# A four-layer graph network on one core: layer 3 planned among layer 2, preparation in two parts, loads by need

## The chip, the cores and the metric

The kernel runs on one core of one Trainium2 chip. The metric is the device time of one execution in microseconds (us); the median of three executions of the kernel before is 1182.61 us.

The core's engines work side by side, each through its own queue in order: TensorE (PE, matmuls, with its weight loads shown as PEld), VectorE (DVE), ScalarE (ACT), GpSimd (POOL) and SyncE (SP), which here only issues transfers (DMAs). TensorE reads from SBUF and writes to PSUM, of which the kernel uses eight banks of 128 x 512 f32.

## The reference, cut to what matters

32 graphs of 512 nodes with 128 features pass through four layers; all graphs share one adjacency matrix, and no graph depends on another. Every layer is `x = x + layer(relu(layernorm(x)))`.

```python
def _L0(x, adj, ...):            # attention over scores of node pairs, softmax over the other axis
    h = x @ others_weight
    ...
    out = einsum('bik,bkl->bil', att, h) + x @ self_weight
def _L1(x, A, ...):              # attention, then an aggregation over A and two dense steps
    h = x @ Wp + bp
    attn = softmax(where(A <= 0, min, leaky(s_src[:, :, None] + s_dst[:, None, :])))
    h_gat = relu(layernorm((attn * A) @ h) * gat_g + gat_b)
    z = ((1 + eps) * h_gat + A @ h_gat) @ W1 + b1
    return relu(relu(layernorm(z) * mlp_g + mlp_b) @ W2 + b2 + h_gat)
def _L2(h, adj, W, a, bias):     # attention
    Wh = h @ W
    attention = softmax(where(adj > 0, leaky(f1[:, :, None] + f2[:, None, :]), NEG))
    return elu(attention @ Wh + bias)
def _L3(x, adj, W, e, bias):     # one matrix for all graphs
    A = softmax(where(adj > 0, e[0][cumsum(adj > 0) - 1], NEG))
    return (A * eye) @ (x @ W[0]) + (A * (1 - eye)) @ (x @ W[1]) + bias
```

Layer 3's matrix A depends on the adjacency and on e alone, not on x. It is computed once, and it needs a long chain: the rank of every edge, the look-up of e by rank, a softmax.

## The kernel before, in words

**A graph.** x stays in SBUF for all 32 graphs (`xs`, 128 partitions x 4 chunks of 128 nodes). `preln` normalises a graph: statistics on VectorE (`st`, `mv`, `nmean`), the reciprocal deviation `rstd` and the scaled `xn` on GpSimd, four transposes on TensorE (`pt`), the relu into `hT` on ScalarE. `layer0` projects (`proj` to `h`), sends a small piece of `h` through four tiny DMAs on SP's queue to bring pair scores to other partitions (`u`), repeats a row (`prow`), takes maxima on VectorE, exponentials on ScalarE, scales (`hs`) and multiplies (`po`). `layer1` and `layer2` share `attend`: row `prow`, four `y` with the mask (line 574, VectorE), a leaky step and an exponential for each (lines 596 and 604, ScalarE), 16 transposes of `y` (line 375, TensorE), copies `pT` and 16 matmuls `po` (line 624). `layer1` goes on with an aggregation over `adjTe` (`pg`, line 795) and two dense steps (`pz`, `px`). `layer3` is short on every engine but TensorE: `own` (line 845), `p` (line 522), four groups of five matmuls (`po`, lines 856 and 860), a sum `yo` and the store of the result.

**The plan.** The order of instructions on each engine isn't written by hand. Every step is given to a `Plan` (line 94) as an operation with an engine, an estimated length and what it reads and writes; operations of one graph in one layer form a chain. `Plan.run` (line 136) simulates the engines with these lengths and emits the operations one by one: of the operations that could begin first on an engine (within `SLACK`), it takes the one with the smallest turn. A chain's turn is its begin, which grows by a `gap` from chain to chain (line 107), plus `STRETCH` times the length of the way to the operation. At most `WINDOW` = 7 chains beyond the oldest unfinished one may run (line 160). Tiles come from rooms with a fixed number of places, the eight PSUM banks among them. The emitted order is binding for each engine (line 194).

**Order of the chains.** The preamble (line 390: loads of x and the adjacency, layer 0's weights, masks), then all 32 graphs of layer 0, all of layer 1, all of layer 2, all of layer 3 (line 1161).

**The preparation.** `prepare` (line 871) makes what the later layers need and no graph owns: the centred weights and score columns of layer 1 and 2, the biases in three bf16 terms (`terms`, line 952), the adjacency with its diagonal (`adjTe`), the parameter rows, and layer 3's matrix: `maskT`, `pn` (line 1017), `num`, `pb` (line 1032), `in_row`, `pg` (line 1083), `pd` (line 1105), the softmax, the transposes `pt_att` into `offT` (line 1152) and the diagonal `pr` into `adiag_rep` (line 1156). It is one chain outside the window, a filler: its turn is `FILLED` = 1e6 for every operation, so that any operation of a graph that can begin at the same time goes first; and it must leave two PSUM banks free.

**Transfers.** SP's queue carries the x loads (eight ahead: `AHEAD`, lines 393 to 397, then one by each layer-0 graph, line 637), the preparation's loads, the four `u` transfers of each layer-0 graph (line 648) and the stores. ScalarE's queue carries three loads at the start (lines 398 to 400). A transfer in the plan takes its issue, a delay of 2.2 and, if it has a `load`, time on one shared bus.

Of the kernel before, what the change touches and what calls it, by code (L numbers as in the profile page):

```python
# [33 lines left out]
P = 128  # L34
# [3 lines left out]

WINDOW = 7

AHEAD = 8


PE, DVE, ACT, POOL, SP, ACTQ = "PE", "DVE", "ACT", "POOL", "SP", "ACTQ"

DELAY = {PE: 0.25, DVE: 0.15, ACT: 0.2, POOL: 0.15, SP: 2.2, ACTQ: 2.2}

SLACK = 0.05

STRETCH = 4.0  # L50

FILLED = 1e6


class Room:
# [29 lines left out]
class Operation:  # L85
    def __init__(self, engine, length, emit, chain, slots):
        self.engine, self.length, self.emit, self.chain, self.slots = engine, length, emit, chain, slots
        self.after, self.missing = [], 0
        self.ready = 0.0
        self.load = 0.0  # L90
        self.way = 0.0


class Plan:
# [7 lines left out]
        self.chains = []  # L102
        self.begin = 0.0

    def chain(self, gap=0.0, filler=False):

        self.chains.append([0, filler, FILLED if filler else self.begin])
        self.begin += gap

    def op(self, engine, length, emit, reads=(), writes=(), load=0.0):  # L110
        slots = list(dict.fromkeys(v.slot for v in (*reads, *writes) if v.slot is not None))
        k = len(self.chains) - 1
        op = Operation(engine, length, emit, k, slots)
        op.load = load
# [12 lines left out]
        for n in needs:  # L127
            n.after.append(op)
            if n.chain == k:
                op.way = max(op.way, n.way + n.length + DELAY[n.engine])  # L130
        op.turn = (self.chains[k][2] + STRETCH * op.way, len(self.ops))
        op.missing = len(needs)
        self.chains[-1][0] += 1
        self.ops.append(op)

    def run(self):
        tc, nc = self.tc, self.tc.nc
        idle = dict.fromkeys(DELAY, 0.0)
        bus = 0.0
        ready = {e: [] for e in DELAY}  # L140
        for op in self.ops:
            if not op.missing:
                ready[op.engine].append(op)
        left = [n for n, _, _ in self.chains]
        normal = [k for k, (_, filler, _) in enumerate(self.chains) if not filler]
        order = {k: i for i, k in enumerate(normal)}
        oldest = 0
        last = {}
        traced = nc.cur_bb.bb.instructions
        seen = len(traced)  # L150
        for _ in range(len(self.ops)):
            while oldest < len(normal) and not left[normal[oldest]]:
                oldest += 1
            best = None
            for engine, ops in ready.items():
                could = []
                for op in ops:
                    k = op.chain
                    filler = self.chains[k][1]
                    if not filler and order[k] >= oldest + WINDOW:  # L160
                        continue
                    begin = max(idle[engine], op.ready)
                    new = [s for s in op.slots if s.tile is None]
                    rooms = {}
                    for s in new:
                        rooms[s.room] = rooms.get(s.room, 0) + 1
                    for room, n in rooms.items():
                        if len(room.free) < n + (room.reserve if filler else 0):
# [12 lines left out]
            ready[op.engine].remove(op)  # L181
            for s in op.slots:
                if s.tile is None:
                    s.room.free.remove(min(s.room.free))
                    s.tile = s.room.make(s.name)
            end = begin + op.length
            idle[op.engine] = end
            done = end + DELAY[op.engine]
            if op.load:
                bus = max(done, bus) + op.load  # L190
                done = bus
            op.emit()
# [25 lines left out]
def kernel(  # L218
# [137 lines left out]

    def load(engine, dst, src, writes, size=0.0):
        q = nc.sync if engine is SP else nc.scalar
        op(engine, 0.45, lambda: q.dma_start(dst(), src), writes=writes, load=size)

    def load_x(b):
        load(SP, lambda: xs[:, b], x[b].rearrange("(c p) f -> p c f", p=P), [v_x[b]], 1.0)
# [27 lines left out]
    plan.chain()  # L390
    wt_o = value(spare, "wt_o")
    v_att = Value()
    load_x(0)
    for ib in range(C):
        load(SP, lambda ib=ib: bias[:, ib, :], adj[blk(ib), :], [v_adj[ib]], 1.0)
    for b in range(1, AHEAD):
        load_x(b)
    load(ACTQ, lambda: wt_o.t[:, 0, :], l0_wo, [wt_o], 0.25)
    load(ACTQ, lambda: att, l0_att.rearrange("(t p) o -> p (t o)", p=P), [v_att])
    load(ACTQ, lambda: wts[:, W_S, :], l0_ws, [v_wts[W_S]], 0.25)  # L400
    v_w0b = Value()
    score_weights(lambda: wt_o.t[:, 0, :], wt_o, att, v_att, w0_ext[:, P:P2], v_w0)
    copy_op(DVE, 0.15, lambda: w0_ext[:, 0:P], lambda: wt_o.t[:, 0, :], [wt_o], [v_w0b])
# [232 lines left out]
    def layer0(b):  # L636
# [12 lines left out]
                        u.own[up * 64 : up * 64 + 64, :, k : k + 1], h[0].t[k:P:2, up:C:2, P + k : P + k + 1]  # L649
                    )  # L650

        op(SP, 1.8, emit_pair, h, [u])
        ls = Value()

        def emit_ls():
# [185 lines left out]
    def layer3(b):  # L841
# [26 lines left out]
        op(SP, 0.5, lambda: nc.sync.dma_start(out[b].rearrange("(c p) f -> p c f", p=P), yo.t), [yo], [Value()])  # L868


    def prepare():
        def dve(length, emit, reads, writes):
            op(DVE, length, emit, reads, writes)

        wt_p, wt_1, wt_l2, row_p, row_1 = (value(spare, n) for n in ("wt_p", "wt_1", "wt_l2", "row_p", "row_1"))
        v_a1, v_a2, v_e, v_eps = Value(), Value(), Value(), Value()

        def line(v):
            return v.rearrange("(p o) -> p o", o=1)
# [14 lines left out]
            load(SP, lambda n=n: mlp_gb[:, n : n + 1], line(v), [v_mlp])  # L894
        for n, v in enumerate((l1_gg, l1_gb, l1_b2, l2_bias, l3_bias)):
            load(SP, lambda n=n: rows[:, n, :], all_rows(v), [v_rows], 0.25)
        for n, w in ((W_2, l1_w2), (W_30, l3_w[0]), (W_31, l3_w[1])):
            load(SP, lambda n=n: wts[:, n, :], w, [v_wts[n]], 0.25)
        load(SP, lambda: e_col, l3_e.rearrange("o (t p) -> p (o t)", p=P), [v_e])
        load(SP, lambda: e_last, l3_e[:, NE - 1 : NE].to_broadcast([P, 1]), [v_e])  # L900

        for ib in range(C):
            dve(0.31, lambda ib=ib: nc.vector.tensor_scalar(
# [67 lines left out]

        dve(0.15, lambda: nc.vector.tensor_scalar(rows[:, B_L2, :], rows[:, B_L2, :], 1.0, None, ALU.add), [], [v_rows])
        dve(0.15, lambda: nc.vector.tensor_scalar(rows[:, B_L3, :], rows[:, B_L3, :], -1.0, None, ALU.add), [], [v_rows])

# [181 lines left out]
        turn_op(lambda k: pr3.t[:, k, :], lambda k: adiag[:, k : k + 1].to_broadcast([P, P]), v_diag, [pr3])  # L1156
        copy_op(ACT, 0.49, lambda: adiag_rep, lambda: wide(pr3.t), [pr3], [v_adiag_rep])

    plan.chain(filler=True)
    prepare()  # L1160
    for layer, gap in ((layer0, 6.6), (layer1, 13.3), (layer2, 7.6), (layer3, 5.9)):
        for b in range(B):
            plan.chain(gap)
            layer(b)
    plan.run()


# [31 lines left out]
```

## Time and profile before

| what | value |
|---|---|
| executions of the kernel before | 1182.61, 1182.65, 1181.53 us |
| the profiled execution | 1182.39 us, of which the span from first to last instruction is 1180.3 us |
| TensorE busy | 1109.0 us (94% of the span) |
| VectorE busy | 961.3 us (81%) |
| ScalarE busy | 665.4 us (56%) |
| GpSimd busy | 670.2 us (57%) |
| mean granted TensorE clock | 0.975 |
| chain of waits that ended last | TensorE 60%, VectorE 28%, ScalarE 4%, GpSimd 3% |
| x load, 256 KB | 32 issues, 4.0 us to landing |
| `u` transfer, 0.5 KB | 128 issues, 1.8 us to landing |

The profile is of one execution. A busy time is the sum of the times in which an engine had an instruction under way; on TensorE neighbouring matmuls overlap, so that the distance from one start to the next tells more than a length. The rows of the slices cut the span into 40 equal parts of 29.5 us and give the busy share of each in tenths. The table of stretches gives, for each engine, the busy time and in brackets the number of instructions; the last three columns are the granted TensorE clock, the share of the DMA engines and GB/s. In a timeline, the bracket at the end of a row is the time in which the engine sat idle before it and what it waited for.

The stages by the timeline: layer 0 to about 243 us, layer 1 to about 747, layer 2 to about 977, layer 3 to the end.

### The profile page before, as it was taken

To read this page: it belongs to the slowest core of one execution; us is meant where nothing else is said; L and a number is where in the kernel's file an instruction comes from. 1 tells how busy PE (TensorE), PEld (TensorE's weight loads), DVE (VectorE), ACT (ScalarE), POOL (GpSimd) and SP (SyncE) were. 2 spreads that over 40 slices of the span, in tenths; PEclk is the share of its full clock that TensorE was granted. 3 is DMA by queue.
4 is the path that set the end of the run, shared out by engine and by line. 5 is a ranking of instruction groups with operands and counts; after the bars stand their busy time and mean duration, and the time that the engine had idled before them with its cause. 6 is when DMAs were issued, how large, how long until landed. Compare 5 with 4: busy or idle time off the path is not lost.

```text
span 1180.3 us, 25261 instructions
## 1 busy us (share of the span) xinstructions
PE 1109.0 (94%) x8682; PEld 1002.6 (85%) x8683; DVE 961.3 (81%) x3854; ACT 665.4 (56%) x1588; POOL 670.2 (57%) x1040
## 2 busy tenths in 40 slices
PE   4899999977999999999999999997999997999998
PEld 3899999976778878788878878697999996999998
DVE  5999999966988898898998888999999997444431
ACT  2555555415747655666556767598999992122221
POOL 5444444530464664645674565746677686777761
PEclk8899999988999999999999999999999997999999
DMA  7111210000000000000000000000000000111111
GB/s 194 29 37 38 46 20 2 2 1 1 2 1 1 2 1 1 2 1 1 2 1 1 2 1 2 1 2 1 2 1 2 2 1 10 46 46 46 46 46 54
DMA packets 56911, 20.50 MB, mean 17 GB/s; under 512 B 21584, under 2 KB 56272, under 8 KB 56784
## 3 DMA queue, kind: packets, MB, share of 16 engines
q1 hardware_dynamic: 56224, 18.76, 6.5%
q8 instruction: 69, 1.13, 0.4%
q14 instruction: 58, 0.48, 0.1%
q10 hardware_dynamic: 560, 0.13, 0.1%
HBM read 10.43 MB, written 8.39 MB: 16 GB/s over the span
## 4 chain that ended last, share of the span: by engine, by line
PE 60%; DVE 28%; ACT 4%; POOL 3%; issue 2%; DMA 2%; SPq 0%; DVEq 0%; ACTq 0%; POOLq 0%
PE po L624 11%; PE po L860 10%; PE pt L375 7%; PE po L749 7%; PE pg L795 6%; DVE y L574 5%; PE proj L544 4%; DVE st L461 4%; DVE pT L368 3%; PE po L856 2%; PE p L522 2%; DVE pT L613 2%; ACT y L604 2%; PE prow L375 2%; PE px L522 2%
## 5 line engine op out<-in xcount | busy, mean ns | idle before, releaser
L624 PE MATMUL po<-h,pT 128*128 128x128 f32 x2048 | 249.5, 278 | 17.3 <-DVE pT L368 14.3
L624 PEld LDWEIGHTS po<-h,pT 128*128 128x128 f32 x2048 | 239.6, 194 | 26.1 <-DVE pT L368 17.6
L497 POOL TENSOR_SCALAR xn<-xs,nmean,rstd 128x128 f32<-128x128 f32 x512 | 229.2, 462 | 46.3 <-DVE yo L867 39.4
L596 ACT ACTIVATE y<-y,h 128x512 f32<-128x512 f32 x256 | 165.5, 718 | 48.6 <-DVE rmax L574 48.4
L604 ACT ACTIVATE y<-y,nmax 128x512 f32<-128x512 f32 x256 | 181.9, 719 | 11.6 <-DVE nmax L587 10.2
L506 ACT ACTIVATE hT<-pt 128x512 f32<-128x512 f32 x128 | 76.0, 595 | 174.2 <-DVE own L845 90.1
L477 POOL TENSOR_TENSOR rstd<-ve,mhalf 128x4 f32<-128x4 f32 x160 | 162.9, 1018 | 13.3
L574 DVE CUSTOM_DVE_ANT_0 y<-prow,bias 128x512 f32<-128x512 f32 x256 | 161.1, 681 | 4.3 <-PE prow L375 4.3
L375 PEld LDWEIGHTS pt<-ident,y 128*128 128x128 f32 x1024 | 115.9, 142 | 34.1 <-ACT y L604 21.0
L375 PE MATMUL pt<-ident,y 128*128 128x128 f32 x1024 | 132.8, 276 | 9.0 <-ACT y L604 7.6
L860 PE MATMUL po<-h,offT 128*128 128x128 f32 x1024 | 136.8, 277 | 0.0
L475 POOL TENSOR_SCALAR ve<-mv 128x4 f32<-128x4 f32 x160 | 34.6, 216 | 167.6 <-DVE mv L463 142.4
L860 PEld LDWEIGHTS po<-h,offT 128*128 128x128 f32 x1024 | 126.3, 194 | 0.0
L795 PE MATMUL pg<-adjTe,hg 128*128 128x512 f32 x256 | 126.2, 593 | 0.0
L544 PE MATMUL proj<-w_ext,hT 128*128 128x130 f32 x768 | 110.2, 283 | 2.0 <-ACT hT L506 1.9
L366 ACT COPY h<-proj 128x260 f32<-128x260 f32 x192 | 66.7, 370 | 79.6 <-PE proj L544 63.2
L461 DVE BATCH_NORM_STATS2 st<-xs 128x6 f32<-128x128 f32 x512 | 110.6, 277 | 0.3 <-DMA xs<-in_x_dram 0.3
L544 PEld LDWEIGHTS proj<-w_ext,hT 128*128 128x128 f32 x768 | 100.1, 198 | 6.9 <-ACT hT L506 3.0
L776 POOL TENSOR_TENSOR rstd<-ve,mhalf 128x4 f32<-128x4 f32 x32 | 32.7, 1023 | 109.2 <-DVE ve L769 102.7
L613 DVE TENSOR_TENSOR pT<-pt,adjT 128x512 f32<-128x512 f32 x128 | 81.3, 680 | 15.5 <-PE pt L375 15.3
L375 PE MATMUL pt<-ident,xn 128*128 128x128 f32 x512 | 86.0, 283 | 5.5 <-POOL xn L497 3.9
L375 PEld LDWEIGHTS pt<-ident,xn 128*128 128x128 f32 x512 | 63.4, 143 | 21.8 <-POOL xn L497 16.2
(190 smaller groups left out, 2135.0 us busy)
## 6 DMA issues: line engine op xcount, KB each, us to landing
xs<-in_x_dram SPq DMA_DIRECT2D x32, 256.0 KB, 4.0
out_dram<-yo SPq DMA_DIRECT2D x32, 256.0 KB, 2.2
u<-h SPq DMA_DIRECT2D x128, 0.5 KB, 1.8
bias<-in_adj_dram SPq DMA_DIRECT2D x4, 256.0 KB, 4.8
wts<-in_L_gnn_W_dram SPq DMA_DIRECT2D x3, 64.0 KB, 2.6
rows<-in_L_gnn_bias_dram SPq DMA_DIRECT2D x2, 64.0 KB, 3.3
wt_o<-L_gnn_others_weight_dram ACTq DMA_DIRECT2D x1, 64.0 KB, 4.7
wts<-n_L_gnn_self_weight_dram ACTq DMA_DIRECT2D x1, 64.0 KB, 5.1
```

Source lines behind the costliest of these rows:

```text
L375: nc.tensor.transpose(dst(k), src(k), ident)
L461: nc.vector.bn_stats(st[:, c, :], src(c))
L477: nc.gpsimd.tensor_tensor(rstd.own, ve, mhalf, ALU.pow)
L497: nc.gpsimd.tensor_scalar(xn.t[:, c, :], src[:, c, :], nmean.own[:, c : c + 1], rstd.own[:, c : c + 1], ALU.add, ALU.mult,)
L544: nc.tensor.matmul(p[:, c, :], lhsT=column(hT, 2 * k + c), rhs=w_ext, start=(b3 is None), stop=(b3 is None or c == 1),)
L574: nc.vector.tensor_tensor_reduce(wide(y[ib].t), wide(prow.t), bias[:, ib, :], 1.0, LOWEST, ALU.add, ALU.max, rmax.own[:, ib : ib + 1],)
L596: nc.scalar.activation(yw, yw, AF.Prelu, alpha=0.2, bias=h[0].t[:, ib, P : P + 1])
L604: nc.scalar.activation(yw, yw, AF.Exp, bias=nmax.own[:, ib : ib + 1], accum_out=ssum[0].own[:, ib : ib + 1])
L613: op(DVE, 0.6, lambda ib=ib, pt=pt, pT=pT: nc.vector.tensor_mul(pT.t, pt.t, weights[:, :, blk(ib)]), [pt, *v_weights], [pT])
L624: nc.tensor.matmul(po[ib].t[:, ib, :], lhsT=pT.t[:, jb, :], rhs=h[0].t[:, jb, 0:P], start=(jb == 0), stop=(jb == C - 1),)
L795: nc.tensor.matmul(wide(pg.t), lhsT=hg.t[:, nb, :], rhs=adjTe[:, nb, :], start=(nb == 0), stop=(nb == C - 1))
L860: nc.tensor.matmul(po[ib].t[:, ib, :], lhsT=offT[:, jb, blk(ib)], rhs=h1.t[:, jb, :], start=False, stop=(jb == C - 1),)
```

## The change

Four things are changed, all of them in what the plan is told; no operation's computation is touched.

1. The chains of layers 2 and 3 are interleaved: layer 3 of graph b follows layer 2 of graph b + 4 (`LAG`), with gaps of 7.0 and 6.0 instead of 7.6 and 5.9.
2. The preparation becomes two chains. `prepare` (all but layer 3's matrix) has the turn `PREPARED` = 40, `prepare_last` (layer 3's weights, e and the matrix) keeps `FILLED`. Neither counts in the window.
3. The loads: the three loads of ScalarE's queue are declared earlier, six graphs of x are loaded ahead instead of eight, and the plan now has eight transfer lanes: a transfer must wait until the one eight before it has landed. The `u` transfers take four lanes, a store takes a lane and time on the bus.
4. The first six chains of graphs are `RAMP` = 4 times as far apart in their begins.

```diff
-AHEAD = 8
+AHEAD = 6
+LANES = 8
-FILLED = 1e6
+PREPARED, FILLED = 40.0, 1e6
+RAMP, LAG = 4.0, 4
...
-    def chain(self, gap=0.0, filler=False):
-        self.chains.append([0, filler, FILLED if filler else self.begin])
+    def chain(self, gap=0.0, turn=None, name=""):
+        self.chains.append([0, turn is not None, self.begin if turn is None else turn, name])
         self.begin += gap
...
-        op.turn = (self.chains[k][2] + STRETCH * op.way, len(self.ops))
+        _, beside, begin, _ = self.chains[k]
+        op.turn = (begin + (0.0 if beside else STRETCH * op.way), len(self.ops))
...
+        lanes = [0.0] * LANES
...
                     begin = max(idle[engine], op.ready)
+                    if op.transfers:
+                        begin = max(begin, lanes[op.transfers - 1])
...
             if op.load:
                 bus = max(done, bus) + op.load
                 done = bus
+            if op.transfers:
+                lanes = lanes[op.transfers :] + [done] * op.transfers
...
+    load(ACTQ, lambda: wt_o.t[:, 0, :], l0_wo, [wt_o], 0.25)
     load_x(0)
+    load(ACTQ, lambda: att, l0_att.rearrange("(t p) o -> p (t o)", p=P), [v_att])
     for ib in range(C):
         load(SP, lambda ib=ib: bias[:, ib, :], adj[blk(ib), :], [v_adj[ib]], 1.0)
+    load(ACTQ, lambda: wts[:, W_S, :], l0_ws, [v_wts[W_S]], 0.25)
     for b in range(1, AHEAD):
         load_x(b)
-    load(ACTQ, lambda: wt_o.t[:, 0, :], l0_wo, [wt_o], 0.25)
-    load(ACTQ, lambda: att, l0_att.rearrange("(t p) o -> p (t o)", p=P), [v_att])
-    load(ACTQ, lambda: wts[:, W_S, :], l0_ws, [v_wts[W_S]], 0.25)
...
-        op(SP, 1.8, emit_pair, h, [u])
+        op(SP, 1.8, emit_pair, h, [u], transfers=4)
...
-        for n, w in ((W_2, l1_w2), (W_30, l3_w[0]), (W_31, l3_w[1])):
-            load(SP, lambda n=n: wts[:, n, :], w, [v_wts[n]], 0.25)
-        load(SP, lambda: e_col, l3_e.rearrange("o (t p) -> p (o t)", p=P), [v_e])
-        load(SP, lambda: e_last, l3_e[:, NE - 1 : NE].to_broadcast([P, 1]), [v_e])
+        load(SP, lambda: wts[:, W_2, :], l1_w2, [v_wts[W_2]], 0.25)
...
+    def prepare_last():
+        v_e = Value()
+        load(SP, lambda: e_col, l3_e.rearrange("o (t p) -> p (o t)", p=P), [v_e])
+        load(SP, lambda: e_last, l3_e[:, NE - 1 : NE].to_broadcast([P, 1]), [v_e])
+        for n, w in ((W_30, l3_w[0]), (W_31, l3_w[1])):
+            load(SP, lambda n=n, w=w: wts[:, n, :], w, [v_wts[n]], 0.25)
...
-    plan.chain(filler=True)
+    plan.chain(turn=PREPARED)
     prepare()
-    for layer, gap in ((layer0, 6.6), (layer1, 13.3), (layer2, 7.6), (layer3, 5.9)):
-        for b in range(B):
-            plan.chain(gap)
-            layer(b)
+    plan.chain(turn=FILLED)
+    prepare_last()
+    order = [(layer0, 6.6, b) for b in range(B)] + [(layer1, 13.3, b) for b in range(B)]
+    for b in range(B + LAG):
+        if b < B:
+            order.append((layer2, 7.0, b))
+        if b >= LAG:
+            order.append((layer3, 6.0, b - LAG))
+    for n, (layer, gap, b) in enumerate(order):
+        plan.chain(gap * RAMP if n < AHEAD else gap, name=layer.__name__)
+        layer(b)
     plan.run()
```

The rest of `prepare` from `maskT` on moves into `prepare_last` unchanged. The changed plan emits the same instructions in the same numbers on each engine; only their order differs.

More of the change, by code (lines that the diff above doesn't have):

```diff
@@ L89, in __init__ @@
         self.ready = 0.0
-        self.load = 0.0
+        self.load, self.transfers = 0.0, 0
         self.way = 0.0
@@ L103, in __init__, with op @@
         self.begin = 0.0
-    def chain(self, gap=0.0, filler=False):
-        self.chains.append([0, filler, FILLED if filler else self.begin])
+    def chain(self, gap=0.0, turn=None, name=""):
+        self.chains.append([0, turn is not None, self.begin if turn is None else turn, name])
         self.begin += gap
-    def op(self, engine, length, emit, reads=(), writes=(), load=0.0):
+    def op(self, engine, length, emit, reads=(), writes=(), load=0.0, transfers=0):
         slots = list(dict.fromkeys(v.slot for v in (*reads, *writes) if v.slot is not None))
@@ L113, in op @@
         op = Operation(engine, length, emit, k, slots)
-        op.load = load
+        op.load, op.transfers = load, transfers
         for s in slots:
@@ L143, in run @@
                 ready[op.engine].append(op)
-        left = [n for n, _, _ in self.chains]
-        normal = [k for k, (_, filler, _) in enumerate(self.chains) if not filler]
+        left = [c[0] for c in self.chains]
+        normal = [k for k, c in enumerate(self.chains) if not c[1]]
         order = {k: i for i, k in enumerate(normal)}
@@ L158, in run @@
                     k = op.chain
-                    filler = self.chains[k][1]
-                    if not filler and order[k] >= oldest + WINDOW:
+                    beside = self.chains[k][1]
+                    if not beside and order[k] >= oldest + WINDOW:
                         continue
                     begin = max(idle[engine], op.ready)
+                    if op.transfers:
+                        begin = max(begin, lanes[op.transfers - 1])
                     new = [s for s in op.slots if s.tile is None]
@@ L167, in run @@
                     for room, n in rooms.items():
-                        if len(room.free) < n + (room.reserve if filler else 0):
+                        if len(room.free) < n + (room.reserve if beside else 0):
                             begin = None
@@ L358, in load @@
         q = nc.sync if engine is SP else nc.scalar
-        op(engine, 0.45, lambda: q.dma_start(dst(), src), writes=writes, load=size)
+        op(engine, 0.45, lambda: q.dma_start(dst(), src), writes=writes, load=size, transfers=1)
     def load_x(b):
@@ L867, in layer3, with dve @@
         op(DVE, 0.6, lambda: nc.vector.tensor_add(yo.t, xb.t, po[0].t), [xb, *po], [yo])
-        op(SP, 0.5, lambda: nc.sync.dma_start(out[b].rearrange("(c p) f -> p c f", p=P), yo.t), [yo], [Value()])
+        op(SP, 0.5, lambda: nc.sync.dma_start(out[b].rearrange("(c p) f -> p c f", p=P), yo.t), [yo], [Value()], load=1.0, transfers=1)
+    def dve(length, emit, reads, writes):
+        op(DVE, length, emit, reads, writes)
     def prepare():
-        def dve(length, emit, reads, writes):
-            op(DVE, length, emit, reads, writes)
         wt_p, wt_1, wt_l2, row_p, row_1 = (value(spare, n) for n in ("wt_p", "wt_1", "wt_l2", "row_p", "row_1"))
-        v_a1, v_a2, v_e, v_eps = Value(), Value(), Value(), Value()
+        v_a1, v_a2, v_eps = Value(), Value(), Value()
         def line(v):
```

## The prediction

> **What bounds the kernel now.** I read the slices of the span first, then the busy time by stage, then TensorE's timeline at the seams. The slices:
>
> ```profile
> PE   4899999977999999999999999997999997999998
> DVE  5999999966988898898998888999999997444431
> ACT  2555555415747655666556767598999992122221
> ```
>
> TensorE is full except at the start, near slices 8 and 9 (layer 0 to 1), through layer 2 and at slice 33 (layer 2 to 3). By stage (us, then busy us of PE, PEld, DVE, ACT, POOL):
>
> ```profile
> 0.00:60.00 60.00, 38.80 (x265) 35.69 (x266) 45.53 (x244) 24.01 (x73) 29.54 (x63) 0.86 0.47 110
> 240.00:320.00 80.00, 65.88 (x443) 56.32 (x443) 59.92 (x215) 41.37 (x95) 21.08 (x28) 0.87 0.00 1
> 740.00:960.00 220.00, 202.99 (x1705) 192.20 (x1705) 211.59 (x703) 198.99 (x452) 150.11 (x224) 0.99 0.01 1
> 960.00:1000.00 40.00, 30.98 (x218) 28.00 (x217) 32.29 (x97) 18.79 (x39) 28.15 (x34) 0.79 0.00 1
> 1000.00:1160.00 160.00, 159.71 (x1433) 159.52 (x1432) 71.35 (x280) 31.35 (x53) 112.38 (x189) 1.00 0.16 47
> ```
>
> In layer 2 (740 to 960) VectorE is 96% busy and TensorE waits; in layer 3 (1000 to 1160) TensorE is full and VectorE 45% busy. TensorE's timeline gives the paces (start, length, operation, count, wait):
>
> ```profile
> 939.79 0.60 PE L375 MATMUL pt<-ident,xn 128*128 128x128 f32 x4
> 940.23 1.91 PE L375 MATMUL pt<-ident,y 128*128 128x128 f32 x16
> 942.41 1.06 PE L544 MATMUL proj<-w_ext,hT 128*128 128x130 f32 x8
> 943.31 3.73 PE L624 MATMUL po<-h,pT 128*128 128x128 f32 x32
> 946.88 0.60 PE L375 MATMUL pt<-ident,xn 128*128 128x128 f32 x4
> ...
> 950.72 1.16 PE L624 MATMUL po<-h,pT 128*128 128x128 f32 x8 [1.05 <-DVE pT L368]
> ...
> 955.28 0.60 PE L375 MATMUL pt<-ident,xn 128*128 128x128 f32 x4
> ...
> 988.84 1.06 PE L375 MATMUL pr<-ident,adiag 128*128 128x128 f32 x4
> 993.18 0.79 PE L856 MATMUL po<-wts,own 128*128 128x128 f32 x2 [3.28 <-DVE own L845]
> ...
> 1024.41 0.60 PE L375 MATMUL pt<-ident,xn 128*128 128x128 f32 x4
> ...
> 1030.21 0.60 PE L375 MATMUL pt<-ident,xn 128*128 128x128 f32 x4
> ```
>
> A layer-2 graph without a wait takes 946.88 - 939.79 = 7.09 us, two take 955.28 - 939.79 = 15.49, so 7.75 each on average; a layer-3 graph takes 5.80. The same rows give unwaited steps: 0.109 us for a transpose, 0.112 for half of a 128-wide f32 matmul; 0.43 for half of a 512-wide one comes from the pg rows. Counting TensorE's instructions in each stretch at such steps gives 1070 us of work in the 1180.3 us span and 110 lost to waits and slow clock: 31.1 before 60 us, 5.9 to 240, 27.1 to 320, 3.6 to 740, 21.5 to 960, 16.9 to 1000, -0.5 to 1160 (rounding of the steps), 4.5 after. The change adds, drops and resizes no instruction on any engine, so the 1070 stay and only the losses move.
>
> **Layer 0 to layer 1 (27.1 lost).** Layer 1 needs its weights and its three-term biases, and the preparation that makes them has the last turn (FILLED), so most of it runs only when layer 0 is out of work:
>
> ```profile
> 255.13 0.59 PE L929 MATMUL pc<-a,bp_rep 128*128 128x2 f32 x2 [4.24 <-DVE row_n L1025]
> 255.58 4.41 PE L1032 MATMUL pb<-row_n,bf 128*128 128x1 f32 x20
> 259.84 0.38 PE L539 MATMUL proj<-b_p,ones 128*128 128x260 bf16 x1
> ```
>
> Layer 0's last po ends at 243 and layer 1's first projection is at 259.84; then all its first graphs wait together for y. In the changed order (how instructions stand on each engine) the weights' matmuls come before layer 0's first po, and layer 1's first projection, row and transposes stand among the last four layer-0 graphs. What can remain: at least 0.7 (80 us at the 3.6 in 420 of layer 1), at most 13 (the waits of 269 to 302 in the PE rows, 7.5, and 5.5 for slow clock). I take 4, nearest to the running layer: -23, bounds -26 and -14.
>
> **The start (31.1 lost).** The price of that is paid here. The first six graphs get due times 26.4 us apart instead of 6.6, so that the weights (turn 40) outrank graph 2 and later. On VectorE the weights' steps that ran at 245 to 262 move up: three centrings 2.3 us, eye 1.2, adjTe 0.8, the terms 2.05 + 1.8, copies 1.0, about 9 us, into a stretch where VectorE is busy 27.8 of 30 us (30 to 60). They stand between NMAX and hs of graph 0, and behind them the next graphs' stats, rows and hs wait. On SP's queue 13 x loads took 12.45 us (0.96 each) ahead of the first weight; now 7 do, so the weights' loads begin about 6 us earlier. But 19 loads (about 0.5 each, 9.5 us) now stand between graph 0's u and graph 1's u. Graph 0's h is ready at 20.3, so its u goes out by 22.9 and graph 1's at about 32.4 (29.06 before), landing near 37. VectorE reaches graph 1's lt only after the weights' 9 us, about 43 by the order, which hides it; without that cover it would cost some 5 us. The first stop, wt_o, stays: its issue waits in both kernels for the fourth adjacency load's lane (7.95), and TensorE begins at 12.8. Fewer x loads ahead (6, not 8) cost nothing, hidden by six graphs of 6.4 us each; without them a graph would wait up to the 4.0 in which a load lands. The planner's new lanes and the booked output transfer issue nothing themselves; they act only through the order. Nine us on VectorE against some 2 idle and fewer early stats: I take +6, bounds -2 (graph 0's po comes earlier) and +14 (9 plus 5 for a stretch at half clock).
>
> **Layers 2 and 3 (37.9 lost from 740 to 1160).** After six layer-2 graphs the changed TensorE order is a fixed round: one layer-2 and one layer-3 graph. TensorE needs 7.09 + 5.80 = 12.89 us for it. Others, by the stage rows: VectorE 7.75 x 0.96 + 5.80 x 0.45 = 10.0, ScalarE 7.0 + 1.1 = 8.1, GpSimd 5.3 + 4.1 = 9.4. So TensorE becomes the bound, and the 0.66 us per layer-2 graph goes. What remains:
> - The switch. Layer 3's matrix (prepare_last) must be ready before the first layer-3 po, and a window of 7 graphs lets layer 2 run only to graph 7 until then. Six graphs still at layer 2's pace lose 6 x 0.66 = 4. Before, its last steps (divide, dg, pt_att, pr, own) lost 14.9 us: from 976.9 to 997.5 only 5.7 of work. The order still has nothing between pr and the first po, so the 3.3 of the 993.18 row stay, while the divides now stand among layer-2 work; the chain from pn to pd, once spread over layer 1, is now compressed here (from the last pn to pr the order holds 72 us of TensorE work at the steps above, and some 66 of VectorE's at its rows' lengths, so neither engine has much to spare for waits). I take 4 + 10 = 14; bounds 7 and 28 (4 + 14.9 + 9 for a chain not covered).
> - The round. [...] In layer 2, with GpSimd 68% busy, em's mean is 0.68, its usual length, and nmean's 0.41. I take 3; bounds 0 and 10.
>
> Term: 14 + 3 - 37.9 = -20.9, bounds -31 and 0. [...]
>
> **Sum.** 6 - 23 - 20.9 = -37.9: span 1142.4. The profiled run took 1182.39, 2.1 over its span, and 0.2 less than the median 1182.61: 1144.7, so 1145.
>
> **Rivals.**
> - Only the first seam gains: the first layer-3 graph holds the window while prepare_last crawls at the last turn, and layer 2 stands still. Terms 6, -23 and about 0: 1165 to 1168. For it: its turn is last and its chain serial; against: 72 us of other TensorE work in the order.
> - All seams close: the bounds -2, -26, -31 give 1124. Against: VectorE's 9 us have to go somewhere.
> - Slower, by the round's ring. ScalarE's order puts layer 2's next y behind this round's first h copy, and that behind 8 po matmuls; so after prow the y are ready in about 3.6 (p 0.89, pt 0.44, 8 of po 1.79, proj 0.45) + 0.4 (h) + 2.5 (four leaky steps) + 0.4 (h) + 2.8 (four exponentials) + 0.4 (hops) = 10.1 us, and TensorE's order needs the last at 12.0 (p, pt, po 3.57, proj 0.89, layer 3's po 4.47, pt, 12 transposes 1.31). The slack is 1.9 us. If the ring is 3.4 longer (hops, GpSimd late with xn), each round takes 14.4 instead of 12.9, 26 rounds give back 39 and the kernel is at 1184; with 4.5 it is 1213. It decides against the change from 14.4 us a round. Against it: ScalarE has 4.8 us free per round.
>
> **How the numbers follow.** Forecast (1130 to 1160) 0.62, only the first seam (1160 to 1178) 0.17, all seams 0.09, slower 0.09, no change 0.03. A measurement tells about 0.2% (2.4 us) from no change. Faster 0.88, same 0.03, slower 0.09. All bounds together span 1124 to 1183; leaving half of each outer case out gives 1126 to 1172.
>
> **What would show it.** Right: layer 1 projections before layer 0's last po; a round near 12.9 us with TensorE 99% busy and VectorE near 78%; one weak stretch of some 15 us at the start of layer 2; first 60 us with a few us less TensorE work. Wrong: a round at 14 us with waits on ACT y; TensorE idle for over 20 us ahead of pt_att; over 45 us lost before 70.

## The result, and the profile after

The changed kernel takes 1195.51 us (four runs, 1193.42 to 1197.77) against 1182.07 us for the kernel before beside it (1181.19 to 1182.65): the ratio is 1.0115, with a 95% interval of 1.0091 to 1.0139. It is slower by 13 us; the forecast was 1145. The profiled execution has a span of 1195.3 us.

The same slices as before, of the changed kernel's page (busy tenths in 40 slices of 29.9 us):

```profile
PE   4799999999999999999999998989998999999897
DVE  6999999978789889889989889976767777777772
ACT  2445454557465654665656854826655555555561
```

TensorE's dip between layer 0 and layer 1 (slices 8 and 9 before) is gone. The dips at slices 24 and 26 are the switch to the mixed layers. In the mixed rounds (from slice 28, 837 us, on) TensorE shows 9 in most slices, but VectorE only 6 or 7 and ScalarE 5 or 6. That alone doesn't show a loss, since a 9 stands for anything from 90%; the stretches do.

By stage (us, then busy us of PE, PEld, DVE, ACT, POOL with the number of instructions, the granted clock, the DMA share, GB/s), the changed kernel:

```profile
0.00:60.00 60.00, 36.87 (x239) 34.21 (x240) 46.24 (x244) 20.95 (x62) 30.85 (x64) 0.86 0.42 101
240.00:320.00 80.00, 78.96 (x621) 70.31 (x619) 66.61 (x257) 52.78 (x121) 38.63 (x52) 1.00 0.00 1
700.00:820.00 120.00, 108.54 (x799) 94.94 (x798) 100.15 (x328) 67.85 (x148) 76.24 (x114) 0.96 0.03 10
900.00:1100.00 200.00, 181.36 (x1520) 176.13 (x1519) 148.43 (x469) 116.34 (x250) 125.19 (x196) 0.97 0.06 18
```

Counting TensorE's instructions at the unwaited steps of the prediction gives this ledger of lost time (stretch of the span minus work):

| stretch, us | lost before | forecast | lost after |
|---|---|---|---|
| 0 to 60 | 31.1 | +6 for the start | 34.8 |
| 60 to 240 | 5.9 | | 12.7 |
| 240 to 320 (seam to layer 1) | 27.1 | 4 | 0.9 |
| 320 to 700 | 3.6 (to 740) | 3.6 | 5.7 |
| 700 to 820 (switch) | | 14 | 20.7 |
| 820 to 880 (first rounds) | | | 1.1 |
| 880 to 1160 (rounds) | | 3 | 42.3 |
| layers 2 and 3 together | 37.9 | 17 | 64.1 |
| 1160 to the end | 4.5 | 4.5 | 7.1 |

In 900 to 1100 TensorE is busy 181 of 200 us, where the forecast had 99%, and no other engine is near full. That speaks for a wait that goes round between engines. The first seam did what was forecast. The span misses the forecast by 53 us (1195.3 against 1142.4), and 39 of them stand in one row: the rounds after 880. (Which steps are taken for TensorE's rarer shapes moves some other rows by a few us; the row of the rounds hardly depends on it.) Who waited there? First TensorE's waits in the whole span (line waited for: us in total, times, longest), then VectorE's from 880 to 1150:

```profile
PE po L635 <- DVE pT L379: 27.3, 19, 2.0
```

```profile
DVE yo L878 <- PE po L871: 42.7, 18, 4.5
DVE own L856 <- ACT hT L517: 23.7, 18, 2.0
```

TensorE waits for VectorE's pT, once a round. VectorE in turn waits each round at two places, for TensorE (yo) and for ScalarE (own). The wait of own is the one that decides in most rounds; the experiments show it. One round in VectorE's timeline (start, length, operation, wait):

```profile
1041.13 0.69 DVE L856 SCALAR_TENSOR_TENSOR own<-pt,adiag_rep 128x512 f32<-128x512 f32 x1 [0.38 <-ACT hT L517]
1041.74 0.68 DVE L848 SCALAR_TENSOR_TENSOR em<-em,v 128x512 f32<-128x512 f32 x1
1042.34 0.68 DVE L379 COPY pT<-pt 128x512 f32<-128x512 f32 x1
...
1044.12 0.92 DVE L500 TENSOR_SCALAR nmean<-mv 128x4 f32<-128x4 f32 x1
...
1046.12 0.17 DVE L500 TENSOR_SCALAR nmean<-mv 128x4 f32<-128x4 f32 x1
1046.20 1.28 DVE L379 COPY pT<-pt 128x512 f32<-128x512 f32 x2
...
1050.11 0.69 DVE L840 TENSOR_TENSOR v<-po,rs 128x512 f32<-128x512 f32 x1
...
1050.90 1.58 DVE L598 SCALAR_TENSOR_TENSOR nmax<-top 128x4 f32<-128x4 f32 x1
1053.94 0.69 DVE L878 TENSOR_TENSOR yo<-xb,po 128x512 f32<-128x512 f32 x1 [1.46 <-PE po L871]
1056.64 0.69 DVE L856 SCALAR_TENSOR_TENSOR own<-pt,adiag_rep 128x512 f32<-128x512 f32 x1 [2.01 <-ACT hT L517]
```

and ScalarE's and GpSimd's rows that belong to it:

```profile
1052.58 0.72 ACT L615 ACTIVATE y<-y,nmax 128x512 f32<-128x512 f32 x1 [1.58 <-DVE nmax L598]
...
1055.42 0.71 ACT L847 ACTIVATE em<-v,minus 128x512 f32<-128x512 f32 x1
1056.03 0.57 ACT L517 ACTIVATE hT<-pt 128x512 f32<-128x512 f32 x1
```

```profile
1043.74 1.26 POOL L859 TENSOR_TENSOR xb<-xs,rows 128x512 f32<-128x512 f32 x1
...
1051.20 1.26 POOL L843 TENSOR_TENSOR v<-v,rows 128x512 f32<-128x512 f32 x1
```

Read it as a ring. VectorE goes from own (1041.13) without a gap to the end of nmax (1052.48): 11.35 us. ScalarE's four exponentials need nmax; behind them in its queue stand em and hT, which ends at 1056.60: 4.02 us and a hop of 0.1. Only then does own of the next round begin, at 1056.64. The round is 1056.64 - 1041.13 = 15.51 us, while TensorE's work in it is 12.89.

Of the 17 rounds from own at 888.74 to own at 1149.64, 14 close in this way: hT follows the exponentials and em on ScalarE without a gap. In the other three (ending at 1041.13, 1072.14 and 1149.64) nmax is not held, so that ScalarE is done earlier, and hT waits for TensorE instead, whose po came late and at a slow clock. One of them is the round from 1025.62: TensorE's row of po, ScalarE's row of hT, and the busy times of the stretch (in the order of the stages above):

```profile
1031.43 3.35 PE L635 MATMUL po<-h,pT 128*128 128x128 f32 x16 [1.95 <-DVE pT L379]
```

```profile
1040.50 0.60 ACT L517 ACTIVATE hT<-pt 128x512 f32<-128x512 f32 x1 [1.08 <-PE pt L386]
```

```profile
1025.62:1041.13 15.51, 13.56 (x105) 13.34 (x105) 10.42 (x36) 8.96 (x20) 9.63 (x15) 0.89 0.00 1
```

There the way goes from own over VectorE's statistics and pT to TensorE's po, through the layer-3 matmuls to the next pt and hT, with a granted clock of 0.89.

Why does own wait for hT, when it doesn't use it? Both read the transposed tile `pt` in one PSUM bank, and in both kernels the one that was planned second waits for the other by a semaphore. In the kernel before, own was planned first, and hT waited for own (28 times, 90.1 us in all):

```profile
1019.25 0.69 DVE L845 SCALAR_TENSOR_TENSOR own<-pt,adiag_rep 128x512 f32<-128x512 f32 x1 [1.44 <-PE pt L375]
```

```profile
1019.98 0.60 ACT L506 ACTIVATE hT<-pt 128x512 f32<-128x512 f32 x1 [2.81 <-DVE own L845]
```

In the changed plan hT comes first, and own waits for it (20 times, 24.5 us in all). The plan itself knows nothing of that semaphore: it believes that both may read at once.

Two rows in the ring are far above their usual length: the first nmean (0.92 instead of 0.17) and nmax (1.58 instead of 0.16). Both end with a GpSimd addition: nmean at 1045.04 and `xb` at 1045.00, nmax at 1052.48 and the addition to `v` at 1052.46. From 880 to 1150 nmean was under way beside such an addition 17 times, and all 17 ended 0.02 to 0.04 us after it. Nmax was held in 12 of the 18 rounds of this stretch (1.38 to 1.59 us).

### The profile page after: what moved, and what is told of

The parts are those of the page before. It is cut to its first block, busy times and chain, and to the rows that moved or that the text cites. A ratio compares the mean times of both kernels' runs of the same rounds, so it can differ in the third digit from the quotient of the medians.

```text
span 1195.3 us, 25180 instructions
## 1 busy us (share of the span) xinstructions
PE 1115.8 (93%) x8683; PEld 1008.2 (84%) x8683; DVE 979.8 (82%) x3854; ACT 668.5 (56%) x1588; POOL 673.4 (56%) x1040
## 5 line engine op out<-in xcount | busy, mean ns | idle before, releaser
L635 PE MATMUL po<-h,pT 128*128 128x128 f32 x2048 | 254.7, 281 | 28.4 <-DVE pT L379 27.3
L635 PEld LDWEIGHTS po<-h,pT 128*128 128x128 f32 x2048 | 243.2, 196 | 34.5 <-DVE pT L379 31.0
L508 POOL TENSOR_SCALAR xn<-xs,nmean,rstd 128x128 f32<-128x128 f32 x512 | 232.1, 468 | 8.4 <-DVE yo L878 1.4
L488 POOL TENSOR_TENSOR rstd<-ve,mhalf 128x4 f32<-128x4 f32 x160 | 163.6, 1023 | 13.3
L555 PE MATMUL proj<-w_ext,hT 128*128 128x130 f32 x768 | 116.2, 289 | 5.3 <-ACT hT L517 5.3
L555 PEld LDWEIGHTS proj<-w_ext,hT 128*128 128x128 f32 x768 | 104.1, 202 | 11.2 <-ACT hT L517 7.5
L849 POOL TENSOR_TENSOR xs<-xs,em 128x512 f32<-128x512 f32 x32 | 41.8, 1307 | 122.8 <-DVE em L848 117.7
L624 DVE TENSOR_TENSOR pT<-pt,adjT 128x512 f32<-128x512 f32 x128 | 81.1, 682 | 11.1 <-PE pt L386 10.5
```

The costliest lines, as they stand in the source:

```text
L488: nc.gpsimd.tensor_tensor(rstd.own, ve, mhalf, ALU.pow)
L508: nc.gpsimd.tensor_scalar(xn.t[:, c, :], src[:, c, :], nmean.own[:, c : c + 1], rstd.own[:, c : c + 1], ALU.add, ALU.mult,)
L555: nc.tensor.matmul(p[:, c, :], lhsT=column(hT, 2 * k + c), rhs=w_ext, start=(b3 is None), stop=(b3 is None or c == 1),)
L624: op(DVE, 0.6, lambda ib=ib, pt=pt, pT=pT: nc.vector.tensor_mul(pT.t, pt.t, weights[:, :, blk(ib)]), [pt, *v_weights], [pT])
L635: nc.tensor.matmul(po[ib].t[:, ib, :], lhsT=pT.t[:, jb, :], rhs=h[0].t[:, jb, 0:P], start=(jb == 0), stop=(jb == C - 1),)
```

## The experiments

Theory A is this ring, closed by own behind hT. Its rivals: B, the two statistics that stand ahead of the last two pT copies make po late, whatever own does; C, GpSimd's additions stretch VectorE's small operations and that alone is the loss. Each run stands beside runs of the kernel before (medians 1181.2 to 1182.1).

**1. Own before hT.** hT is made to depend on own; the plan is made anew.

```diff
-        hT, pt = preln(b)
         own = value(by_dve, "own")
-        op(DVE, 0.6, ... own ..., [pt, v_adiag_rep], [own])
+        hT, _ = preln(b, diagonal)    # diagonal(pt) adds own; hT then reads [pt, own]
```

> Theory A (a ring through two queues): in the changed kernel's round own and hT read the same transposed tile, and own (VectorE) waits until hT (ScalarE) has read it; hT stands on ScalarE behind the four exponentials of the round, and these wait for nmax at the end of VectorE's round. So VectorE's round from own to nmax (949.51 to 959.5, about 10.0 us) and ScalarE's from the first exponential to hT (959.54 to 963.57, about 4.0 us) run one after the other: 14.1 a round, where TensorE needs 12.89. Here own is put first and hT behind it; all else is the changed kernel. A expects rounds of 12.9 to 13.2, no own that waits for hT, and 42 us of loss from 880 to 1160 shrunk to 5 to 12: 1158 to 1167. Rival B (the two STATS that stand ahead of the last two pT copies make po late, whatever own does): rounds stay near 14, 1188 to 1198. Rival C (GpSimd's adds stretch nmean, 0.7 us a round): rounds of 14 less at most 0.7.

Measured: 1154.16 us, ratio 0.9775 (0.9759 to 0.9791). TensorE's round, from one graph's xn transposes to the same place a round later, and the stretch that answers to the last one above:

```profile
910.43 0.60 PE L386 MATMUL pt<-ident,xn 128*128 128x128 f32 x4
...
923.32 0.60 PE L386 MATMUL pt<-ident,xn 128*128 128x128 f32 x4
```

```profile
900.00:1100.00 200.00, 200.00 (x1803) 200.00 (x1802) 159.41 (x567) 129.87 (x290) 150.58 (x230) 1.00 0.08 22
```

12.89 us, exactly the forecast round, and TensorE is busy 200 us of 200. From 820 to 1120 the ledger shows no loss at all. But the plan also came out in another order: the three pT copies stand together, and em and the statistics behind them. So this run takes away B's cause too, and the holds with it (the first nmean takes 0.28 us):

```profile
928.47 0.28 DVE L500 TENSOR_SCALAR nmean<-mv 128x4 f32<-128x4 f32 x1
```

It doesn't tell A from B or C; experiment 5 parts the wait from the order.

**2. Layers apart, and 3. mixing alone.** The changed kernel with layer 2 for all graphs and then layer 3; and the kernel before with the mixing only.

```diff
-    for b in range(B + LAG): ...                       # 2: on the changed kernel
+    order += [(layer2, 7.6, b) for b in range(B)] + [(layer3, 5.9, b) for b in range(B)]
-    for layer, gap in ((layer0, 6.6), ...):            # 3: on the kernel before
+    order = ...; for b in range(B + 4): layer2 of b, layer3 of b - 4
```

> The changed kernel with layer 2 for all graphs and then layer 3, with the gaps of before (7.6 and 5.9); the two-part preparation, the loads and the spaced first graphs stay. If the mixing makes the whole loss (A, B and C alike), the 64.1 lost from 700 to 1160 go back to the 37.9 of before: 1195.5 - 26.2 = 1169, with 1165 to 1180 since layer 3's matrix now comes at the last turn. If the loss comes from the two-part preparation or the loads, the time stays at 1190 to 1200.

> The kernel before with the one change that layers 2 and 3 are mixed as in the changed kernel; the preparation stays one chain at the last turn, loads and first graphs as before. All theories that blame the round: 1182.1 - 37.9 + 64.1 = 1208, with the seam from layer 0 to layer 1 still open. If the switch (20.7 lost from 700 to 820) comes from giving layer 3's matrix the last turn in a chain of its own, less: 1195 to 1202.

Measured: 1168.81 us, ratio 0.9900 (0.9885 to 0.9915), and 1208.89 us, ratio 1.0238 (1.0221 to 1.0255). Both agree to a microsecond with what the ledger gives (1169, 1208), so the terms add: the preparation in two parts with the loads is worth -12 us, the mixing as planned costs 28, together +15 against the +13 measured for the whole change.

**4. No nmean.** GpSimd subtracts the mean itself.

```diff
-        nc.vector.tensor_scalar(nmean.own, mv[:, :, 0], -1.0, None, ALU.mult)
-   xn: src + nmean.own[c], * rstd    (ALU.add, ALU.mult)
+   xn: src - mv.own[c, 0], * rstd    (ALU.subtract, ALU.mult)
```

> The changed kernel without VectorE's nmean: GpSimd's xn subtracts the mean instead of adding its negative, so the result is the same. In the round the first nmean took 0.91 us (952.49 to 953.40, while GpSimd's add ran until 953.38) and the second 0.17. If the first is held by GpSimd's add, and the ring of A is what sets the round, about 1.0 us of the ring of 14.1 goes: rounds of 13.1 to 13.3, some 19 us less in the 20 rounds after 880, and about 1 us in layers 0 and 1: 1172 to 1180. If TensorE's waits do not come from VectorE's round (the ring is not there), rounds stay at 14.1 and 1190 to 1196. If what nmean waited for is simply waited for by the next operation, the same: no gain but the 0.17s.

Measured: 1253.14 us, ratio 1.0623 (1.0589 to 1.0657), a miss. The cause stands in the groups of the page (count, then busy us and mean ns), first the changed kernel, then this run:

```profile
L508 POOL TENSOR_SCALAR xn<-xs,nmean,rstd 128x128 f32<-128x128 f32 x512 | 232.1, 468 | 8.4 <-DVE yo L878 1.4
```

```profile
L502 POOL TENSOR_SCALAR xn<-xs,mv,rstd 128x128 f32<-128x128 f32 x512 | 422.3, 836 | 5.4 <-DVE res L820 0.6
```

The xn step itself nearly doubled, 190 us more on GpSimd. The run says nothing on nmean.

**5. Own before hT, every queue as it was.** After the plan is made, its order is kept on every engine; only own is put ahead of hT in the program (28 graphs of layer 3), so that the semaphore points the other way.

```diff
+        hT.relu.behind = op(DVE, 0.6, ... own ..., [pt, v_adiag_rep], [own])
+   after planning: emit in the planned order of each engine, with own ahead of hT
```

> In the run with own first the plan also came out in another order (three pT copies together, em and the STATS behind them), so it does not tell the wait from the order. Here every engine executes exactly the changed kernel's instructions in exactly its order; only for 28 of the 32 layer-3 graphs hT now waits for own instead of own for hT. By theory A own then runs in the idle time behind yo (948.75 instead of 949.51), and the next thing that binds VectorE is em, which waits for ScalarE's em (done 948.90, so VectorE's at about 949.3 instead of 950.12): the ring is 0.8 shorter, rounds of 13.4 instead of 14.2, 20 rounds, 16 us: 1175 to 1183. If the order alone counts (theory B), 1190 to 1197. If the wait alone made the whole loss, rounds of 12.9: 1158 to 1165.

Measured: 1170.62 us, ratio 0.9897 (0.9880 to 0.9915). The same part of VectorE's timeline:

```profile
1000.43 0.69 DVE L931 TENSOR_TENSOR yo<-xb,po 128x512 f32<-128x512 f32 x1 [2.83 <-PE po L924]
1001.03 0.68 DVE L909 SCALAR_TENSOR_TENSOR own<-pt,adiag_rep 128x512 f32<-128x512 f32 x1
1001.63 0.68 DVE L900 SCALAR_TENSOR_TENSOR em<-em,v 128x512 f32<-128x512 f32 x1
...
1010.78 0.21 DVE L650 SCALAR_TENSOR_TENSOR nmax<-top 128x4 f32<-128x4 f32 x1
1013.83 0.69 DVE L931 TENSOR_TENSOR yo<-xb,po 128x512 f32<-128x512 f32 x1 [2.84 <-PE po L924]
```

The round is 13.40, as theory A gave it: own runs at once behind yo. The time fell by 25 instead of the 12 to 20 expected, because I had taken 14.2 for the changed kernel's round, from one stretch; its mean from 871 to 1149 is 277.5 / 18 = 15.4. Nmax is at 0.21 here: with the wait its hold went too. Turning the wait round is thus worth 25 us, the hold of nmax among them, and the new order of run 1 another 16. B as the main cause falls, since every queue has its old order.

The 13.40 came by another link than expected, though. Em follows own without a wait. What closes the round is VectorE's yo, which waits 2.84 us for TensorE's po, while TensorE waits for pT:

```profile
1006.82 2.05 PE L687 MATMUL po<-h,pT 128*128 128x128 f32 x16 [0.25 <-DVE pT L431]
```

That pT stands behind the two statistics: from yo (1000.43) over own, em, the statistics and pT to this po VectorE's part is 6.39 us, from there to the next yo (1013.83) TensorE's is 7.01, together 13.40. So the half us that is left above 12.89 comes by rival B's link, and the number expected for the round was in part luck.

**6. Nmean on GpSimd, the same plan.** GpSimd adds as before and makes the negative mean itself.

```diff
-            nc.vector.tensor_scalar(nmean.own, mv[:, :, 0], -1.0, None, ALU.mult)
+            nc.gpsimd.tensor_scalar(nmean, mv.own[:, :, 0], -1.0, None, ALU.mult)   # in norm()
```

> GpSimd's xn with a subtraction took 0.79 us instead of 0.47 a piece, which spoiled the run without nmean. Here GpSimd adds again, and the negative mean is made by GpSimd itself (one small operation more, 0.2 us); VectorE loses its nmean and the order of all else is the changed kernel's. If VectorE's round is in the ring, each round loses the 0.91 + 0.17, less what xn comes later: rounds of 13.2 to 13.6 instead of 14.2, 20 rounds, 12 to 20 us: 1175 to 1184. If the 0.74 that the first nmean waited beside GpSimd's add only moves to VectorE's next operation, 0.3 a round remain: 1188 to 1194.

Measured: 1160.89 us, ratio 0.9811 (0.9793 to 0.9828), 35 us less than the changed kernel. Rounds of 13.3 to 13.4, as expected, but from 15.4 and not from 14.2: the length of nmean (1.1 a round) is only half of what went, since nmax is no longer held either (0.22 us). Some 3 us were already gained by 320 us.

**9. Nmax ahead of v.** All else in the changed kernel's order; in 18 rounds VectorE's top and nmax change places with rs and v.

```diff
+                if ops[i].kind == "v" and ops[i + 1].kind == "nmax":
+                    ops[i], ops[i + 1] = ops[i + 1], ops[i]
```

> The changed kernel's instructions in its order on every engine, but in 18 rounds VectorE's top and nmax go ahead of rs and v, not behind them. In most of the changed kernel's rounds nmax took 1.58 us (1050.90 to 1052.48) where 0.19 is its usual length, and it ended with GpSimd's add of v (1051.20 to 1052.46), which v itself had released. If GpSimd's add holds nmax, and nmax is in the ring, then a round of 15.5 loses the 1.25 and the 0.87 of rs and v: rounds of 13.3 to 13.5, 18 rounds, 36 us: 1155 to 1165. If nmax was merely slow for another reason (its order alone counts), only the 0.87 goes: 1176 to 1182. If the ring is not there, 1190 to 1197.

Measured: 1167.85 us, ratio 0.9885 (0.9870 to 0.9899), 28 us less. One tile's instructions (count, then ns shortest, median, longest) from 880 to 1140, the changed kernel and this run:

```profile
L598 DVE SCALAR_TENSOR_TENSOR nmax<-top x17: 163/1582/1591, 882.1 to 1128.4; 128x4 f32<-128x4 f32 x17
```

```profile
L655 DVE SCALAR_TENSOR_TENSOR nmax<-top x18: 161/228/233, 893.4 to 1127.7; 128x4 f32<-128x4 f32 x18
```

Nmax is no longer held in this stretch. The round is 13.9, 0.4 to 0.6 above what I expected, and the time 3 us above the range: one h copy (0.35) stands between the leaky steps and the exponentials on ScalarE, which before had run while nmax was held, and now it is in the ring. So C is half right: the holds are real, and this run parts nmax's from the wait of own, which stays. But they aren't the whole loss: in run 5 the first nmean is still held (0.92), and the round is 13.40. The gains of runs 5, 6 and 9 (25, 35 and 28 us) overlap and must not be added, since the hold of nmax is gone in all three.

**7. Layer 3's matrix at turn 450** instead of last, on top of run 1 (`plan.chain(turn=450.0)`).

> Own first (the first experiment) and layer 3's matrix at turn 450, so that its preparation spreads over layer 1 instead of the start of layer 2. In the first experiment 22 us were lost from 700 to 820. If the preparation's own chain makes that loss, it falls to 8 to 15 with up to 4 more in layer 1 (where the kernel before, with the chain there, lost 3.6): 1141 to 1151. If the loss comes from the first layer-2 graphs alone, 1151 to 1157.

Measured: 1147.19 us, ratio 0.9700 (0.9685 to 0.9716). From 700 to 820 the ledger lost 17.5 instead of the 24.8 of run 1 (not the 8 to 15 expected), and from 320 to 700 7.4 instead of 6.3. The preparation's own chain made part of the switch, not all.

**10. The weights at turn 150** instead of 40, on top of run 1 (`PREPARED = 150.0`).

> Own first (the first experiment), and the weights of layer 1 at turn 150 instead of 40; the loads and the spaced first graphs stay. By 120 us the first experiment had lost 45.1 us of TensorE time and the kernel before 35.5, with VectorE equally busy in all (101.9 of 120). If the weights' 9 us on VectorE among the first graphs are the price, the loss by 120 falls to 36 to 40, and some of it comes back where the weights run then: by 320 us 43 to 50, total 1148 to 1156. If the spaced first graphs or the loads are the price, the loss by 120 stays at 43 to 46 and the total at 1152 to 1158.

Measured: 1158.02 us, ratio 0.9802 (0.9786 to 0.9818), no gain. The loss by 120 us fell only from 45.1 to 43.2 (35.5 before the change). But the run doesn't settle what it was made for, because the weights' steps moved only within the first 120 us. The last of layer 1's biases, in run 1 and here:

```profile
40.52 0.23 DVE L967 CAST b<-b_c 128x128 bf16<-128x128 f32 x1
```

```profile
69.01 0.23 DVE L967 CAST b<-b_c 128x128 bf16<-128x128 f32 x1
```

VectorE is about as busy in these 120 us as in run 1 (101.0 us against 101.9). Whether VectorE's nine us, the spaced graphs, the loads or their order make the start stays open.

**8, 11, 12. Versions meant to beat both.** Own first, nmean on GpSimd and an earlier matrix together, with other numbers for the plan.

> A version meant to beat both kernels: own first, layer 3's matrix at turn 600, nmean on GpSimd, a window of 8 graphs. Rounds of 12.9, the switch at 8 to 15 instead of 22, and VectorE some 0.2 us shorter in each of 128 STATS, of which perhaps 5 us show at the start, where VectorE is full: 1133 to 1148. If the later xn on GpSimd (0.2 each) costs what VectorE gains, 1143 to 1153.

> The combined version (own first, nmean on GpSimd, layer 3's matrix early) with other numbers for the plan: window 9, lag 5, eight x loads ahead, weights at turn 100, matrix at turn 700, layer 1's gap 13.7, and VectorE's, ScalarE's and GpSimd's lengths in the plan as the traces have them (nmax 0.47, rs and v 0.88, leaky 0.63, rstd 1.38, xn 1.93). The combined version lost 58 before 880 and 12 at its end; longer planned lengths keep VectorE's order nearer to what runs. Expected 1120 to 1134; if the window of 9 only moves the waits to the banks, 1134 to 1145.

> As the run before it, but window 9 with lag 4, seven x loads ahead, first graphs at 3 gaps, weights at turn 60, matrix at turn 600, and a plan that knows that ScalarE and VectorE read a tile of one bank one after the other. Expected 1120 to 1134; 1134 to 1145 if the plan's knowledge of the reads moves nothing.

Measured: 1134.08 us, 0.9592 (0.9577 to 0.9608); 1126.61 us, 0.9537 (0.9522 to 0.9551); 1129.70 us, 0.9561 (0.9545 to 0.9577). Number 11 is the fastest, 55 us below the kernel before and 69 below the changed one. It still mixes the layers, with rounds of 12.9 throughout.

## Why the prediction was wrong, by its own steps

- **Seam to layer 1 (-23).** Right: 27.1 became 0.9, which is -26, the better end of the range. TensorE is busy 78.96 of 80 us there, and run 2 shows that this gain survives alone.
- **The start (+6).** Size inside its bounds: 3.7 more to 60 us and 6.8 more from there to 240, 10.5 in all. I put it down to the weights on VectorE. That is not shown: run 10 left them among the first graphs. It fits that VectorE waits only 1.1 us in all from 20 to 120 us in the changed kernel, although graph 1's u goes out at 35.0 (29.1 before, 32.4 forecast).
- **The switch (14).** Measured 20.7, inside 7 to 28. Its split into waiting graphs and the matrix's chain holds as far as run 7 shows it: the chain is worth some 7.
- **The round (3, bounds 0 to 10).** This step failed: 42.3 us were lost from 880 to 1160. I took the busy sums of a round (TensorE 12.89, VectorE 10.0, ScalarE 8.1, GpSimd 9.4) and let the largest set the pace. No run shows the 3 or its bound of 10, which were my estimate: the changed kernel lost the 42.3, run 1 nothing from 820 to 1120. The sums were about right, and in run 1 the round is 12.89. But sums lie beside each other only if no queue waits for the other inside the round. In the changed order VectorE's stretch from own to nmax and ScalarE's from the first exponential to hT are in series, 11.4 + 4.1, because own waits for hT. With that wait turned round and every queue as it was, 25 us came back (run 5); with nmax moved, 28 (run 9).
- **The slower rival** (a round's ring, deciding from 14.4 us a round, 1184 to 1213) came true in place and threshold, with a mean round of 15.4. That its price holds too (1195.5) is partly luck: 18 rounds were so long, not 26. And it came through another link: I traced ScalarE's y to TensorE, found 1.9 us of slack, and did not trace VectorE's queue. Its sign, waits for ScalarE's y, was therefore wrong; TensorE waited for VectorE's pT (27.3 us) instead, and for y only 4.9. I gave it 0.09.
- **What could have been read beforehand.** The row of own before shows it waiting for pt alone, and hT waiting for own. The changed order shows hT ahead of own. I used that order for TensorE and ScalarE, and did not ask of each VectorE instruction what it would wait for.
- **VectorE's rows beside GpSimd.** I went by em's row, which stayed at 0.68 in layer 2. Em was the wrong row: GpSimd waits for em (its addition to `xs` starts at 1042.50, after em's end at 1042.42) and so has no addition under way then. In the changed kernel, from 880 to 1150, the first nmean of each round took 0.91 to 0.93 us instead of 0.17 beside a GpSimd addition (17 of 17), nmax 1.38 to 1.59 instead of 0.16 in 12 of 18 rounds. The second nmean of each round ran at 0.17 beside GpSimd's power of 128x4. Before the change one could see nmean at 1.26 from 972.11 on, beside GpSimd's `xb` from 972.06 to 973.34, where its median is 0.17, and nmax at 1.27 beside a median of 0.16.

```profile
L587 DVE SCALAR_TENSOR_TENSOR nmax<-top x26: 161/163/1271, 761.4 to 954.8; 128x4 f32<-128x4 f32 x26
```

I had looked at em and nmean, not at nmax, which stands at the one place where a delay reaches ScalarE at once (nmax ends at 1052.48, the first exponential begins at 1052.58).

## What to carry to other kernels

When two queues are mixed into a round, don't stop at busy sums: follow one round through each in-order queue and look for a path that leaves an engine and comes back, here own, nmax, exponentials, hT, own (15.51 us, where TensorE's busy sum is 12.89). A wait between two readers of one tile is easy to miss, since no data passes (own behind hT: 23.7 us from 880 to 1150); a planner that doesn't know of it may put the readers in the wrong order. A small operation that is held inside such a ring lengthens the round: nmax took up to 1.59 us here in rounds of 15.5, and in run 9, with nmax at 0.23 and ahead of rs and v (0.87), the round was 13.9.

## What the runs showed of the hardware

- In the changed kernel a 128x4 VectorE operation of 0.16 us was held up to 1.59 us, until a GpSimd addition of 128x512 ended, even where VectorE's instruction began 0.3 us ahead of that addition (nmax, 1050.90 and 1051.20), while one of GpSimd's xn pieces was still running. In two rounds with the same neighbours within 0.03 us nmax took only 0.34 and 0.16 (945.01 and 959.29); what decides isn't shown. The second nmean of each round took its 0.17 us while GpSimd's power of 128x4 was under way (1046.12 beside 1045.38 to 1046.40). VectorE's pT copies of 128x512, which read PSUM, stayed at 0.68 in 19 cases beside GpSimd additions of that size (`xs` in 17, `xb` in two).
- GpSimd's 128x128 step with a subtraction and a product, its scalars taken from `mv`, took 0.84 us on average (run 4), and with an addition and a product, from `nmean`, 0.47 (the changed kernel). Which of the two differences makes it was not parted.
- In some of the changed kernel's rounds in which TensorE waited for 2 us its granted clock fell too: 0.90 from 916.80 to 933.98, where hT still followed ScalarE's exponentials without a gap, so that the slow clock cost that round nothing; and 0.89 from 1025.62 to 1041.13, where 16 po took 3.35 us instead of 2.05 and hT waited 1.08 for TensorE.
